# One-head attention layer: denominators, scores and masked weights placed on other engines

## The chip, the core and the metric

The kernel runs on one core of a Trainium2 chip. The metric is device time in microseconds, taken as the median of several runs. A profiled execution is one more execution, recorded by the hardware profiler; its own time is given beside that of the runs.

The engines' names in the profile: PE is TensorE (matmul), PEld its weight loads, DVE is VectorE, ACT is ScalarE, POOL is GpSimd, and SP is the engine that issues most of the plain transfers.

## The reference

Four graph attention layers follow one another on 3327 nodes with 512 features. Each is residual: `x = x + GAT(relu(layernorm(x)))`. The layers have 8, 4, 1 and 8 heads. The one that matters here is the third, with one head:

```python
h = features @ W                       # 512 x 512
s1, s2 = h @ a1, h @ a2                # own score, neighbour's score
e = leaky_relu(s1[:, None] + s2[None, :], 0.2)
e = where(adjacency > 0, e, -9e15)
h_prime = softmax(e, axis=1) @ h
out = elu(h_prime)
```

The adjacency matrix is the same in all layers and sparse: about 17 neighbours per node, with a tail of nodes that have more.

## The kernel before, in words

**Tiling.** Nodes are padded to 3328 and ranked by their number of neighbours, so that they make 26 tiles of 128 nodes (`NT = 26`). A first stage reads the adjacency matrix, finds each node's neighbours and their ranks, and computes the first layer's features. Then the four layers run in `tile_gat_lists`. Each keeps a table in HBM, with one row of 528 numbers for each node: the features, its own score and its neighbour's score.

**Two ways of averaging.** In the one-head layer the nine tiles with most neighbours are *dense*: class `Wholes` treats all 26 source tiles for three target tiles at a time (`wide` is 384 columns), in three rounds `p` with 26 source tiles `j` each. The other 17 are *list* tiles: class `Tile` gathers the rows of the neighbours by indirect DMA from POOL (`gather`, line 835), in groups of up to four (`GROUP`), and VectorE accumulates the weighted rows (line 912).

**A list tile's group.** `fetch` issues the gathers, five groups ahead (`LOOK = 5`, and as many buffers g). `scored` makes the weights: at a tile's first group the own score is copied into `self.s` (line 886); then VectorE adds it to the neighbours' scores (line 888) and takes the leaky relu (line 890), and ScalarE the exponential (line 891). `group` accumulates. After a tile's last group come `divisors`, `means`, and then the tile's end (`ends`): ELU in `bent` and `added` (lines 948 to 964), centring and squares on ScalarE (970, 973), the root on POOL (431), transposes (451), the projection onto the next layer's weights (469), and the table row's store.

**A dense source tile.** Since exp of a leaky relu is the larger of two exponentials, the weight of a source j for a target c is `c_j * max(b_j/c_j * a_c, 1)` up to a factor of the target. The code computes it as a relu with a scale and a bias, plus a constant:

```python
r = self.r[p, j] = pools["o"].tile([P, wide], F32, name="r")                    # PSUM, one buffer
nc.scalar.activation(r, self.a[p], AF.Relu, scale=b, bias=mc)                   # line 1128
...
nc.vector.scalar_tensor_tensor(self.e[p, j], self.r.pop((p, j)), self.c[:, j:j + 1],
                               self.mk.pop((p, j)), OP.add, OP.mult)            # line 1135
```

Then `products` multiplies the masked weights em with the source tile's features on TensorE (line 1162), into one PSUM bank for each of the three target tiles. The denominators take another way: POOL adds two masked weight tiles (`paired`, line 1148), VectorE folds one or two such pairs into a running sum (`added`, line 1154), and after the last source tile TensorE multiplies the sum by a column of ones (`divisors`, line 1169). `means` takes the reciprocal (1173), and `Whole.means` scales the three banks (1089).

**What sets the order.** The engines' instruction order in the layers is written out by hand: a loop over steps (one per list group, 72 in this layer) in which pieces are put with `later(step, place, piece)`. A step has the places "first", "scored" (with the next group's scores), then the group itself, then "last". `Wholes.place` spreads the 26 source tiles of a round over 19 of 21 steps, so that some steps hold two. Each engine executes its own instructions in this order. The transfers by SP are in the order of the same pieces, except that they wait for their buffers.

The functions that the change touches, and what calls them:

Of the kernel before, what the change touches and what calls it, by code (L numbers as in the profile page):

```python
# [10 lines left out]
F32 = mybir.dt.float32  # L11
U8 = mybir.dt.uint8
BF16 = mybir.dt.bfloat16
I32 = mybir.dt.int32
AF = mybir.ActivationFunctionType
OP = mybir.AluOpType
AX = mybir.AxisListType

P = 128
SLOPE = 0.2  # L20
# [5 lines left out]
BANK = 512  # L26
# [8 lines left out]
ROW = 528  # L35
GROUP = 4
DENSE = [0, 1, 9, 3]
ND = max(DENSE)
# [342 lines left out]
class Weights:  # L381
# [19 lines left out]
    def fold(self):  # L401

        if not self.left:
            return
        nc, HF = self.nc, self.HF
        s, k = self.left.pop(0)
        prod = self.work.tile([P, 2 * HF], F32, name="prod", bufs=1)
        nc.vector.tensor_mul(prod.rearrange("p (s n) -> p s n", s=2), self.w[:, k, :, :HF],
                             self.av[:, s, :].rearrange("p (s n) -> p s n", s=2))
        nc.vector.tensor_reduce(self.w[:, k, s, HF:HF + self.H],  # L410
                                prod.rearrange("p (h d) -> p h d", d=self.D), AX.X, OP.add)


def centred(nc, xt, small, work):
# [382 lines left out]
def tile_gat_lists(ctx: ExitStack, tc: tile.TileContext, x, adj, ws, avs, out, ident, half, slots, L, low, spare, tabx, tabs):  # L797
# [7 lines left out]
    nc = tc.nc  # L805
    NP, F = x.shape
    NT = NP // P
# [15 lines left out]
    wide = 3 * P  # L823
# [5 lines left out]
    one, zero = [spool.tile([P, 1], F32, name=n, bufs=1) for n in ("one", "zero")]  # L829
# [16 lines left out]
    class Tile:  # L846
# [29 lines left out]
        def scored(self, i):  # L876

            H = HEADS[self.l]
            t = self.t
            k0, n, g = self.groups[i]  # L880
            if i == 0:
                self.po = pools["o"].tile([P, BANK], F32, name="bank")
                pw = next(scores)
                K = CAPS[t]
                self.wt, self.s = pw[:, :K * 8].rearrange("p (k h) -> p k h", h=8), pw[:, K * 8:K * 8 + H]
                nc.vector.tensor_copy(self.s, g[:, n, F:F + H] if self.l == 0 else g[:, 0, F // 2:F // 2 + H])
            z = small.tile([P, GROUP, 8], F32, name="z")[:, :n, :H]
            nc.vector.tensor_tensor(z, g[:, :n, ROW - 8:ROW - 8 + H],  # L888
                                    self.s.unsqueeze(1).to_broadcast([P, n, H]), OP.add)
            nc.vector.scalar_tensor_tensor(z, z, SLOPE, z, OP.mult, OP.max)  # L890
            nc.scalar.activation(self.wt[:, k0:k0 + n, :H], z, AF.Exp)  # L891
            if self.l == 0:
                ranks = n - (i == 0)
                nc.scalar.activation(slots(t, max(k0, 1), count=ranks), g[:, :ranks, F // 2], AF.Copy)
                if i == 0:
                    nc.scalar.activation(xs[self.t], g[:, n, :F], AF.Copy)
# [30 lines left out]
        def divisors(self):  # L927
            H, K = HEADS[self.l], CAPS[self.t]
            den = self.den = small.tile([P, 8], F32, name="den")
            nc.vector.tensor_reduce(den[:, :H], self.wt[:, :K, :H].rearrange("p k h -> p h k"), AX.X, OP.add)  # L930
            nc.vector.tensor_scalar_max(den[:, :H], den[:, :H], TINY)
            nc.vector.reciprocal(den[:, :H], den[:, :H])
# [151 lines left out]
    class Whole(Tile):  # L1084


        def means(self):
            self.y = low[:, self.t % 3 * F:(self.t % 3 + 1) * F]
            nc.vector.tensor_scalar(self.y, self.po, self.den, None, OP.mult)

    class Wholes:


        def __init__(self, l, W):
            self.l, self.tiles = l, [Whole(l, t, W) for t in range(ND)]
            self.s = pools["e"].tile([P, ND], F32, name="s", bufs=1)
            for t in range(ND):
                nc.sync.dma_start(self.s[:, t:t + 1], tabs[l % 2][t * P:(t + 1) * P, F // 2:F // 2 + 1])
            self.b, self.c, self.mc = [pools["e"].tile([P, NT], F32, name=n, bufs=1) for n in ("b", "c", "mc")]

            self.a = [low[:, 5 * F + p % 2 * wide:5 * F + (p % 2 + 1) * wide] for p in range(ND // 3)]
            self.v, self.e, self.mk, self.r, self.pairs, self.parts = {}, {}, {}, {}, {}, {}

        def targets(self, p):

# [4 lines left out]
            nc.scalar.activation(self.a[p], pa[:, :3, :], AF.Exp, scale=1.0 - SLOPE)  # L1110

        def load(self, p, j):
            v = self.v[p, j] = pools["e"].tile([P, ROW], F32, name="ve", bufs=4)
            nc.sync.dma_start(v, tabs[self.l % 2][j * P:(j + 1) * P, :])
            mk = self.mk[p, j] = pools["e"].tile([P, wide], U8, name="mk", bufs=3)
            nc.sync.dma_start(mk.bitcast(I32), masks[p, j])

        def weights(self, p, j):
            if p == ND // 3:
                return  # L1120
            b, c, mc = [t[:, j:j + 1] for t in (self.b, self.c, self.mc)]
            if p == 0:
                d = self.v[p, j][:, ROW - 8:ROW - 7]
                nc.scalar.activation(b, d, AF.Exp)
                nc.scalar.activation(c, d, AF.Exp, scale=SLOPE)
                nc.scalar.activation(mc, c, AF.Copy, scale=-1.0)
            r = self.r[p, j] = pools["o"].tile([P, wide], F32, name="r")
            nc.scalar.activation(r, self.a[p], AF.Relu, scale=b, bias=mc)

        def masked(self, p, j):  # L1130

            if j % 2 == 0:
                self.two = pools["e"].tile([P, 2, wide], F32, name="em", bufs=3)
            self.e[p, j] = self.two[:, j % 2, :]
            nc.vector.scalar_tensor_tensor(self.e[p, j], self.r.pop((p, j)), self.c[:, j:j + 1],  # L1135
                                           self.mk.pop((p, j)), OP.add, OP.mult)
            if j % 2:
                self.pairs[p, j // 2] = self.two

        def part(self, p, i):  # L1140
            if (p, i) not in self.parts:
                self.parts[p, i] = pools["e"].tile([P, 3, wide], F32, name="parts", bufs=2)
            return self.parts[p, i]

        def paired(self, p, i):

            two = self.pairs.pop((p, i))
            nc.gpsimd.tensor_tensor(self.part(p, i // 2)[:, 1 + i % 2, :], two[:, 0, :], two[:, 1, :], OP.add)

        def added(self, p, i):  # L1150

            parts = self.part(p, i // 2)[:, i < 2:2 + i % 2, :]
            out_ = self.a[p] if i == NT // 2 - 1 else self.part(p, i // 2 + 1)[:, 0, :]
            nc.vector.tensor_reduce(out_, parts.rearrange("p j c -> p c j"), AX.X, OP.add)

        def products(self, p, j):
            e, v = self.e.pop((p, j)), self.v.pop((p, j))
# [5 lines left out]
                                 v.rearrange("p (s m) -> p s m", s=2)[:, :, :F // 2],  # L1163
                                 start=(j == 0), stop=(j == NT - 1))

        def divisors(self, p):
            self.pd = pools["t"].tile([P, F // P, P], F32, name="pt")
            for q in range(3):
                nc.tensor.matmul(self.pd[:, 0, q:q + 1], self.a[p][:, q * P:(q + 1) * P], one, start=True, stop=True)

        def means(self, p):
            den = small.tile([P, 3], F32, name="den3")
            nc.vector.reciprocal(den, self.pd[:, 0, :3])
            for q in range(3):
                tl = self.tiles[3 * p + q]
                tl.den = den[:, q:q + 1]
                tl.means()

        def place(self, n):

            per = n // (ND // 3)
            for p in range(ND // 3):
                s0 = p * per
                later(s0 - 4 if p else -1, "first", lambda p=p: self.targets(p))
                for j in range(NT):
                    s = s0 + j * (per - 2) // NT
                    later(max(s - 3, -1), "first", lambda p=p, j=j: self.load(p, j))

                    if (p, j) == (0, 0):
                        later(-1, "scored", lambda: self.weights(0, 0))  # L1190
                    later(s, "first", lambda p=p, j=j: (self.masked(p, j), self.weights(*divmod(p * NT + j + 1, NT))))
                    later(s + 1, "first", lambda p=p, j=j: self.products(p, j))
                    if j % 2:
                        i = j // 2
                        later(s + 1, "first", lambda p=p, i=i: self.paired(p, i))
                        if i % 2 or j == NT - 1:
                            later(s + 2, "last", lambda p=p, i=i: self.added(p, i))
                later(s + 3, "first", lambda p=p: self.divisors(p))
                later(s + 3, "last", lambda p=p: self.means(p))
                for q in range(3):  # L1200
                    self.tiles[3 * p + q].ends(s + 3 + q)
# [149 lines left out]
    def later(s, place, piece):  # L1351
        at.setdefault((s, place), []).append(piece)
# [128 lines left out]
```

## Time and profile before

| what | value |
|---|---|
| median of three runs | 2442.68 us (2439.82 to 2448.11) |
| the profiled execution's own time | 2959.5 us |
| its span, first to last instruction | 2957.8 us |
| mean granted TensorE clock | 0.867 |
| TensorE, VectorE, ScalarE, POOL busy in the whole span | 2224.7, 1914.3, 931.8, 1728.5 us |
| accumulation in the one-head layer (line 912), first to last start | 1861.8 to 2277.4 us |
| dense products in it (line 1162), first to last start | 1858.9 to 2230.4 us |

The profiled execution takes longer than the runs. Durations below come from it alone. A line of groups gives the source line, engine, operation, output and inputs, shapes and count; after the first bar the busy time of the group in us and the mean of one in ns; after the second the idle time of the engine just ahead of these instructions and what ended it. An fp32 matmul appears as two records. A line of waits reads "who waited <- for whom: us in total, times, longest".

### The profile page before, as it was taken

The numbers are of one execution on the slowest core, as the hardware profiler recorded it, in microseconds if no ns is written. First come the engines' busy times: TensorE is split into PE (matmuls) and PEld (weight loads), VectorE is DVE, ScalarE is ACT, GpSimd is POOL, SyncE is SP. The second block draws the span as 40 slices with busy tenths as digits, with TensorE's granted clock in tenths as the row PEclk, the third lists the DMA queues.
The fourth block names the chain that finished last, engine by engine and source line by source line (L and its number), as shares of the span: only waits on it lengthen the run. The fifth ranks groups of instructions, "written<-read, shape, count | busy, mean of one in ns | idle before, by whom it ended". The sixth has DMA issues, their size and how long they took to land.

```text
span 2957.8 us, 27080 instructions
## 1 busy us (share of the span) xinstructions
PE 2224.7 (75%) x7082; PEld 1251.4 (42%) x7082; DVE 1914.3 (65%) x4968; ACT 931.8 (32%) x2502; POOL 1728.5 (58%) x1717
## 2 busy tenths in 40 slices
PE   4777677787677745788877787689696778877887
PEld 2664243343333323344434344245354445444453
DVE  7887656565546523767765565698887556666665
ACT  5882122222221101323332222344333333333330
POOL 7894465565556663555655552676764555555554
PEclk9988788888888877899988889799897889988898
DMA  6885477677666675666766663788775666666664
GB/s 229 322 294 160 140 218 216 193 235 222 188 205 195 189 194 170 181 202 192 209 193 189 192 192 111 226 264 257 236 248 152 191 177 184 185 182 194 185 187 137
DMA packets 260730, 594.20 MB, mean 201 GB/s; under 512 B 103699, under 2 KB 121107, under 8 KB 256214
## 3 DMA queue, kind: packets, MB, share of 16 engines
q0 software_dynamic: 124368, 432.13, 49.8%
q1 hardware_dynamic: 132454, 153.45, 16.5%
q10 hardware_dynamic: 3744, 6.82, 0.7%
q8 instruction: 57, 0.93, 0.1%
q14 instruction: 107, 0.88, 0.1%
HBM read 542.60 MB, written 49.65 MB: 200 GB/s over the span
## 4 chain that ended last, share of the span: by engine, by line
DVE 21%; PE 18%; issue 16%; another core or an unknown queue 11%; ACT 6%; POOL 4%; DMA 3%; DVEq 0%; ACTq 0%; POOLq 0%; SPq 0%
PE bank L924 11%; DVE m L919 9%; POOL g L835 3%; PE pv L469 3%; PE whole L1310 3%; DVE bank L912 2%; DMA g<-tab,idxb 1%; DVE z L890 1%; DVE z L888 1%; ACT r L1276 1%; DVE x L962 1%; DVE q L439 1%; ACT pw L891 1%; DVE room L1292 1%
## 5 line engine op out<-in xcount | busy, mean ns | idle before, releaser
L924 PE MATMUL bank<-m,ident 128*128 128x512 f32 x2414 | 1236.5, 659 | 268.9 <-DVE m L919 137.5
L835 POOL DMA_INDIRECT g<-tab,idxb x712 | 678.2, 952 | 465.5 <-issue 189.3
L919 DVE TENSOR_TENSOR m<-g,pw 128x512 f32<-128x512 f32 x1207 | 752.0, 682 | 267.6 <-ACT pw L891 193.5
L924 PEld LDWEIGHTS bank<-m,ident 128*128 128x128 f32 x2414 | 490.2, 211 | 879.8 <-issue 568.9
L469 PE MATMUL pv<-w,hT 128*128 128x264 f32 x1664 | 447.4, 423 | 107.0 <-ACT hT L458 71.2
L835 POOL DMA_INDIRECT g<-tabx,twiceb x342 | 324.1, 948 | 245.8 <-issue 124.4
L835 POOL DMA_INDIRECT g<-tab,idxa x297 | 283.1, 953 | 262.1 <-DMA tab<-v 88.5
L469 PEld LDWEIGHTS pv<-w,hT 128*128 128x128 f32 x1664 | 339.5, 208 | 215.2 <-ACT hT L458 79.6
L891 ACT ACTIVATE pw<-z 128x32 f32<-128x32 f32 (+4 forms) x356 | 67.8, 190 | 945.4 <-DVE z L890 509.8
L1162 PE MATMUL whole<-ve,em 128*128 128x512 f32 x468 | 224.5, 632 | 48.2 <-DVE em L1135 27.9
L1310 PE MATMUL whole<-L,room 128*128 128x130 f32 x1248 | 171.1, 288 | 79.2 <-issue 79.0
L1310 PEld LDWEIGHTS whole<-L,room 128*128 128x128 f32 x1248 | 163.1, 201 | 107.1 <-issue 104.7
L695 POOL TENSOR_TENSOR key<-a,keys 128x3328 int32<-128x3328 int32 (+1 forms) x29 | 189.5, 6539 | 15.9 <-DVE cand L704 12.6
L912 DVE SCALAR_TENSOR_TENSOR bank<-g,L,bank 128x512 f32<-128x512 f32 x243 | 183.3, 754 | 9.9 <-remote 2.0
L835 POOL DMA_INDIRECT g<-tabx,twicea x99 | 94.4, 954 | 119.6 <-issue 75.3
L1162 PEld LDWEIGHTS whole<-ve,em 128*128 128x128 f32 x468 | 92.8, 203 | 158.7 <-issue 114.6
L451 PE MATMUL pt<-ident,xn 128*128 128x128 f32 x416 | 74.5, 302 | 93.0 <-issue 32.2
L704 DVE MAX8 cand<-key 128x8 f32<-128x208 int32 x416 | 143.6, 363 | 0.1
L890 DVE SCALAR_TENSOR_TENSOR z<-z 128x32 f32<-128x32 f32 (+5 forms) x428 | 82.5, 193 | 91.4 <-remote 61.4
L919 DVE TENSOR_TENSOR bank<-g,pw 128x512 f32<-128x512 f32 x74 | 51.5, 696 | 126.7 <-ACT pw L891 105.6
L1276 ACT ACTIVATE r<-low,L 128x384 f32<-128x384 f32 x208 | 121.2, 582 | 9.8 <-remote 3.9
L888 DVE TENSOR_TENSOR z<-g,pw 128x32 f32<-128x32 f32 (+4 forms) x356 | 61.8, 174 | 94.9 <-DMA g<-tab,idxa 39.0
(181 smaller groups left out, 2154.4 us busy)
## 6 DMA issues: line engine op xcount, KB each, us to landing
a<-in_adj SPq DMA_DIRECT2D x25, 1664.0 KB
tab<-v SPq DMA_DIRECT2D x78, 264.0 KB
ve<-tab SPq DMA_DIRECT2D x78, 264.0 KB
g<-tab SPq DMA_DIRECT2D x65, 264.0 KB
tabx<-vx SPq DMA_DIRECT2D x26, 528.0 KB
g<-tab,idxb POOLq DMA_INDIRECT x712
low<-tab SPq DMA_DIRECT2D x52, 132.0 KB
spare<-tab SPq DMA_DIRECT2D x52, 132.0 KB
```

The source lines that it names most:

```text
L469: nc.tensor.matmul(pv[:, s, :HF + 8], hT[:, k, :], W.w[:, k, s, :], start=(k == 0), stop=(k == KC - 1))
L695: nc.gpsimd.tensor_tensor(key[:, c:c + quarter], a[:, c:c + quarter], keys[:, c:c + quarter], OP.mult)
L704: nc.vector.max(cand[:, g * 8:(g + 1) * 8], key[:, g * SEG:(g + 1) * SEG])
L835: nc.gpsimd.indirect_dma_start(out=out_, out_offset=None, in_=table, in_offset=bass.IndirectOffsetOnAxis(ap=which, axis=0))
L890: nc.vector.scalar_tensor_tensor(z, z, SLOPE, z, OP.mult, OP.max)
L891: nc.scalar.activation(self.wt[:, k0:k0 + n, :H], z, AF.Exp)
L912: nc.vector.scalar_tensor_tensor(acc, v, w, acc, OP.mult, OP.add)
L919: nc.vector.tensor_tensor(out_.rearrange("p (s h d) -> p s h d", s=2, d=D), v.rearrange("p s (h d) -> p s h d", d=D), wt[:, k0 + q, :H].re ...
L924: nc.tensor.matmul(self.po, ident, m[:, q, :], start=False, stop=(k0 + q == K - 1), skip_group_check=True)
L1162: nc.tensor.matmul(tl.po.rearrange("p (s m) -> p s m", s=2), e[:, q * P:(q + 1) * P], v.rearrange("p (s m) -> p s m", s=2)[:, :, :F // 2], ...
L1276: nc.scalar.activation(self.r[:, h, :], self.a[:, g, :], AF.Relu, bias=-1.0, scale=self.b[:, j, g:g + 1])
L1310: nc.tensor.matmul(dst, e[:, h, q * P:(q + 1) * P], mov, start=False, stop=(j == NT - 1), skip_group_check=True)
```

## The change

There are six edits. All but the first are in the one-head layer.

- When the weights of that layer are folded, a second score column is made beside each: the neighbour's score times 0.2 and the own score times 0.8. The factor `exp(0.2 * own)` cancels in the softmax, so the leaky relu becomes one operation, `max(s2 + 0.8*s1, 0.2*s2)`. It replaces two.
- The copy of the own score goes from VectorE to ScalarE.
- `Whole.means` goes from VectorE to ScalarE.
- ScalarE writes the dense weights straight into the SBUF pairs em (four pairs, where there were three), and VectorE adds and masks them in place. The PSUM buffer r is gone.
- VectorE's running sums are gone. Each pair sum from POOL is multiplied by the column of ones on TensorE, and accumulates in a PSUM bank of its own, which takes the place of r.
- Rows and masks of a source tile are loaded four steps ahead and not three, with five buffers each (four and three before).

```diff
@@ fold
+        if self.H == 1:
+            nc.vector.tensor_scalar(self.w[:, k, s, HF + 1:HF + 2], self.w[:, k, s, HF:HF + 1],
+                                    SLOPE if s else 1.0 - SLOPE, None, OP.mult)
@@ scored
-                nc.vector.tensor_copy(self.s, g[:, n, F:F + H] if self.l == 0 else g[:, 0, F // 2:F // 2 + H])
+                if H == 1:
+                    nc.scalar.activation(self.s, g[:, 0, F // 2 + 1:F // 2 + 2], AF.Copy)
+                else:
+                    nc.vector.tensor_copy(self.s, g[:, n, F:F + H] if self.l == 0 else g[:, 0, F // 2:F // 2 + H])
             z = small.tile([P, GROUP, 8], F32, name="z")[:, :n, :H]
+            if H == 1:
+
+                nc.vector.scalar_tensor_tensor(z, g[:, :n, ROW - 8:ROW - 7], self.s, g[:, :n, ROW - 7:ROW - 6],
+                                               OP.add, OP.max)
+                nc.scalar.activation(self.wt[:, k0:k0 + n, :H], z, AF.Exp)
+                return
@@ Whole.means
-            nc.vector.tensor_scalar(self.y, self.po, self.den, None, OP.mult)
+            nc.scalar.activation(self.y, self.po, AF.Copy, scale=self.den)
@@ Wholes.__init__
+            bank = pools["o"].tile([P, BANK], F32, name="pd")
+            self.pd = [bank[:, 8 * p:8 * p + 3] for p in range(ND // 3)]
@@ load
-            v = self.v[p, j] = pools["e"].tile([P, ROW], F32, name="ve", bufs=4)
+            v = self.v[p, j] = pools["e"].tile([P, ROW], F32, name="ve", bufs=5)
...
-            mk = self.mk[p, j] = pools["e"].tile([P, wide], U8, name="mk", bufs=3)
+            mk = self.mk[p, j] = pools["e"].tile([P, wide], U8, name="mk", bufs=5)
@@ weights, masked
-            r = self.r[p, j] = pools["o"].tile([P, wide], F32, name="r")
-            nc.scalar.activation(r, self.a[p], AF.Relu, scale=b, bias=mc)
+            if j % 2 == 0:
+                self.made = pools["e"].tile([P, 2, wide], F32, name="em", bufs=4)
+            self.e[p, j] = self.made[:, j % 2, :]
+            nc.scalar.activation(self.e[p, j], self.a[p], AF.Relu, scale=b, bias=mc)
+            if j % 2:
+                self.pairs[p, j // 2] = self.made
...
+            e = self.e[p, j]
+            nc.vector.scalar_tensor_tensor(e, e, self.c[:, j:j + 1], self.mk.pop((p, j)), OP.add, OP.mult)
@@ paired, added
-            nc.gpsimd.tensor_tensor(self.part(p, i // 2)[:, 1 + i % 2, :], two[:, 0, :], two[:, 1, :], OP.add)
+            self.sums[p, i] = pools["e"].tile([P, wide], F32, name="sums", bufs=3)
+            nc.gpsimd.tensor_tensor(self.sums[p, i], two[:, 0, :], two[:, 1, :], OP.add)
...
-            nc.vector.tensor_reduce(out_, parts.rearrange("p j c -> p c j"), AX.X, OP.add)
+            both = self.sums.pop((p, i))
+            for q in range(3):
+                nc.tensor.matmul(self.pd[p][:, q:q + 1], both[:, q * P:(q + 1) * P], one, start=(i == 0 and q == 0),
+                                 stop=(i == NT // 2 - 1), skip_group_check=True)
@@ divisors (removed), means
-                nc.tensor.matmul(self.pd[:, 0, q:q + 1], self.a[p][:, q * P:(q + 1) * P], one, start=True, stop=True)
...
-            nc.vector.reciprocal(den, self.pd[:, 0, :3])
+            nc.vector.reciprocal(den, self.pd[p])
@@ place
-                    later(max(s - 3, -1), "first", lambda p=p, j=j: self.load(p, j))
+                    later(max(s - 4, -1), "first", lambda p=p, j=j: self.load(p, j))
...
-                        if i % 2 or j == NT - 1:
-                            later(s + 2, "last", lambda p=p, i=i: self.added(p, i))
-                later(s + 3, "first", lambda p=p: self.divisors(p))
+                        later(s + 3, "first", lambda p=p, i=i: self.added(p, i))
                 later(s + 3, "last", lambda p=p: self.means(p))
```

More of the change, by code (lines that the diff above doesn't have):

```diff
@@ L1101, in __init__ @@
             self.a = [low[:, 5 * F + p % 2 * wide:5 * F + (p % 2 + 1) * wide] for p in range(ND // 3)]
-            self.v, self.e, self.mk, self.r, self.pairs, self.parts = {}, {}, {}, {}, {}, {}
+            self.v, self.e, self.mk, self.pairs, self.sums = {}, {}, {}, {}, {}
+            bank = pools["o"].tile([P, BANK], F32, name="pd")
+            self.pd = [bank[:, 8 * p:8 * p + 3] for p in range(ND // 3)]
         def targets(self, p):
@@ L1126, in weights @@
                 nc.scalar.activation(mc, c, AF.Copy, scale=-1.0)
-            r = self.r[p, j] = pools["o"].tile([P, wide], F32, name="r")
-            nc.scalar.activation(r, self.a[p], AF.Relu, scale=b, bias=mc)
-        def masked(self, p, j):
[L1132 to L1143, printed above, removed]
+            if j % 2 == 0:
[4 more added lines that the diff above has]
+                self.pairs[p, j // 2] = self.made
+        def masked(self, p, j):
+            e = self.e[p, j]
+            nc.vector.scalar_tensor_tensor(e, e, self.c[:, j:j + 1], self.mk.pop((p, j)), OP.add, OP.mult)
         def paired(self, p, i):
             two = self.pairs.pop((p, i))
-            nc.gpsimd.tensor_tensor(self.part(p, i // 2)[:, 1 + i % 2, :], two[:, 0, :], two[:, 1, :], OP.add)
+            self.sums[p, i] = pools["e"].tile([P, wide], F32, name="sums", bufs=3)
+            nc.gpsimd.tensor_tensor(self.sums[p, i], two[:, 0, :], two[:, 1, :], OP.add)
         def added(self, p, i):
-            parts = self.part(p, i // 2)[:, i < 2:2 + i % 2, :]
-            out_ = self.a[p] if i == NT // 2 - 1 else self.part(p, i // 2 + 1)[:, 0, :]
-            nc.vector.tensor_reduce(out_, parts.rearrange("p j c -> p c j"), AX.X, OP.add)
+            both = self.sums.pop((p, i))
+            for q in range(3):
+                nc.tensor.matmul(self.pd[p][:, q:q + 1], both[:, q * P:(q + 1) * P], one, start=(i == 0 and q == 0),
+                                 stop=(i == NT // 2 - 1), skip_group_check=True)
         def products(self, p, j):
@@ L1164, in products @@
                                  start=(j == 0), stop=(j == NT - 1))
-        def divisors(self, p):
-            self.pd = pools["t"].tile([P, F // P, P], F32, name="pt")
-            for q in range(3):
-                nc.tensor.matmul(self.pd[:, 0, q:q + 1], self.a[p][:, q * P:(q + 1) * P], one, start=True, stop=True)
         def means(self, p):
             den = small.tile([P, 3], F32, name="den3")
-            nc.vector.reciprocal(den, self.pd[:, 0, :3])
+            nc.vector.reciprocal(den, self.pd[p])
             for q in range(3):
```

## The prediction

> **What bounds the kernel now.** The edits lie in the third of four layers (the one with one head) and in a fold of its weights, so I first cut that layer out. The engine sums by stretch show it: it starts when the last rows of its table have landed (about 1850 us), its vector work ends near 2285. The next layer cannot begin its gathers before, so what ends this layer earlier ends the kernel earlier by as much.
>
> ```profile
> core 0: us, PE busy (x) PEld busy (x) DVE busy (x) ACT busy (x) POOL busy (x), PEclk, DMA share, GB/s
> 1850.00:2285.00 435.00, 338.70 (x1004) 191.68 (x1005) 358.67 (x728) 169.40 (x410) 289.15 (x307) 0.89 0.77 235
> ...
> 2020.00:2060.00 40.00, 40.00 (x134) 24.14 (x135) 32.05 (x64) 15.68 (x32) 25.78 (x28) 1.00 0.88 272
> 2140.00:2180.00 40.00, 40.00 (x142) 25.68 (x141) 30.26 (x63) 16.10 (x32) 25.05 (x28) 1.00 0.75 233
> 2100.00:2120.00 20.00, 9.97 (x33) 6.21 (x34) 18.56 (x36) 6.08 (x14) 10.14 (x11) 0.76 0.68 201
> 2240.00:2260.00 20.00, 9.42 (x31) 7.40 (x32) 17.95 (x45) 8.46 (x20) 14.15 (x16) 0.67 0.66 177
> ```
>
> VectorE is busy 359 of 435 us, TensorE 339, ScalarE 169. Two kinds of stretch alternate: where three dense tiles end (2100, 2240) VectorE is full and TensorE half idle at a low clock; after the first of these ends (2020, 2140) TensorE is full, catching up, and VectorE waits. POOL's 289 hides the pause between gathers, which is why I count it by hand. Next, the groups of the layer's window, for durations and counts:
>
> ```profile
> L1162 PE MATMUL whole<-ve,em 128*128 128x512 f32 x468 | 224.5, 632 | 48.2 <-DVE em L1135 27.9 <-issue 13.9 <-DVE low L1089 6.4
> L912 DVE SCALAR_TENSOR_TENSOR bank<-g,L,bank 128x512 f32<-128x512 f32 x243 | 183.3, 754 | 9.9 <-remote 2.0 <-DVE bank L912 1.2
> ...
> L1135 DVE SCALAR_TENSOR_TENSOR em<-r,c,mk 128x384 f32<-128x384 f32 x78 | 47.8, 612 | 24.8 <-issue 10.1 <-ACT r L1128 8.5 <-ACT hT L458 4.8
> L1148 POOL TENSOR_TENSOR parts<-em 128x384 f32<-128x384 f32 x39 | 39.3, 1007 | 0.8
> L1154 DVE TENSOR_REDUCE parts<-parts 128x384 f32<-128x1152 f32 x15 | 22.0, 1467 | 0.0
> ...
> L1089 DVE TENSOR_SCALAR low<-whole,den 128x512 f32<-128x512 f32 x9 | 6.2, 744 | 0.1
> ```
>
> TensorE waits for the masked weights (L1135), and these stand in VectorE's queue behind reductions (L1154) that nothing needs before the tiles end. Last, the waits, to see who holds whom:
>
> ```profile
> ACT r L1128 <- DVE em L1135: 75.2, 36, 5.5
> ```
> ```profile
> POOL root L431 <- DVE ve L978: 33.8, 12, 8.3
> ...
> POOL g L835 <- DVE bank L912: 13.1, 9, 3.4
> ```
>
> ScalarE waits 75 us for its single PSUM buffer r; POOL waits for VectorE. Both point at VectorE as the pace.
>
> **POOL's floor.** In the timeline a gather takes 0.95 us and the next follows 0.30 later. The layer has 243: 304 us. Its 39 pair sums at 1.00 + 0.17 are 46, its 26 roots at 0.56 + 0.17 are 19. Sum 369. The gathers run from 1849.3 to 2264.7, 415 us. So POOL has 46 us of slack, spent on waits for VectorE; no relief of VectorE alone can bring more than that in the profiled execution.
>
> [...] with one PSUM operand L912 takes 756 ns, with two SBUF operands L962 takes 692, both on 512 elements. [...] The masked weights become such an operation. [...] L956, with two SBUF inputs, has a median of 690 ns with one case of 2108, the gathers a median near 950 with a maximum of 1364. [...]
>
> **The change part by part**, against the profiled execution's own 2959.5 us.
>
> *Running sums.* 21 reductions leave VectorE: 22.0 + 2.9 + 2.9 (18 and 3 of them, 1.47 us wide and 0.95 narrow) = 27.8 us. In their place TensorE multiplies each of 39 pair sums by ones, three products each, and nine at the ends go: 36 groups of three more. The nine in the trace (L1169) took 0.80 us per three at the full clock and 1.41 at a low one. So TensorE gains 29 to 51 us; I take 29, because they fall mostly in busy stretches. That is work on an engine with 96 us idle, but in the 80 us where TensorE is full it is paid: 80/435 of 29, 5 us.
>
> *Scores.* 72 groups lose one of two small operations. Their median is 157 ns (L888), start to start 0.2: 11 to 14 us off VectorE, taken as 11. The own-score copy (17 at 144 ns) goes to ScalarE: 2.4 us off.
>
> *Dense means.* Nine at 0.69 to 0.74 us: 6.2 us off VectorE. ScalarE gets nine at about 0.70 (its L476, from PSUM with a scale) and 17 small copies at 0.19: 9.5 us on an engine 39% busy. If that cover were gone the next tile's first product would be late by 2 us, three times.
>
> *Weights into SBUF pairs.* ScalarE no longer waits for r. VectorE idled 8.5 us on r and 10.1 unexplained before L1135, chiefly when one step holds two source tiles; I count 12 of these 19. Duration of the in-place operation: by the 64 ns above, 5 us less over 78; [...] taking L956's mean of 795 over its median, 8 us more. I take nothing. ScalarE's write to SBUF is not in the trace in this form; against the present 675 ns its neighbours to SBUF give 614 to 706 for 512 elements, so between -5 and +5 us on an engine with room.
>
> *Loads.* The same 78 rows and 78 masks, issued one step earlier with five buffers of each. On SP's queue a row load still waits for a product about three steps before its use, and own rows and table stores behind it wait no longer. ScalarE waits 27.9 us on rows, 13.6 of it once at the start, which an earlier issue does not move as they hang on the table. Nothing counted.
>
> *New waits.* TensorE's small products stand at step s + 3, products of later source tiles behind them; they wait for POOL's pair sum of step s + 1. VectorE had this wait before at s + 2, and lost 2.1 us in 21 reductions. *Folds:* eight operations of about 0.15 us in the first layer, 1.2 us, beside TensorE's sums there.
>
> *Sum.* VectorE: 27.8 + 11 + 2.4 + 6.2 = 47.4 busy, 12 idle, 59 in all. Only the 355 of 435 us in which TensorE is not full can profit: 48; less 5 for the added products: 43. POOL's slack of 46 cannot be used whole, since each root still waits for VectorE and each gather for a buffer; three quarters of 43 is 32. This quarter is my judgement. What is late next: POOL at 369 and TensorE at 339 + 29 = 368, both in about 400.
>
> So 2959.5 becomes about 2927. The median of the runs is 2442.7, 517 us less than the profiled execution; the trace doesn't say where. Shrunk by that ratio, the layer would have 359 us, exactly VectorE's busy time, so VectorE is there at least as much the bound. I take off the same 32 us, unscaled: 2410.
>
> **Rivals.** (a) *POOL or TensorE takes over at once.* If POOL's pauses and waits stay, or the added products cost 51 us, 10 to 18 us remain: about 2428. For it: TensorE would be 92% busy. Against it: its clock rises as it fills. (b) *The layer runs free,* if unprofiled gathers are quicker: 47 busy plus all 19 idle, less 8 for TensorE: 2385. (c) *Slower: TensorE held by POOL.* A gather step puts four gathers (5 us) and perhaps a root ahead of the pair sum. If POOL stands more than two steps (2 x 5.9 us) behind TensorE, each of 39 small groups holds the products, then SP's row loads, then the masks. TensorE has 96 - 29 = 67 us of idle left: a mean hold over 1.7 us decides. At 2.4 us, 39 x 2.4 - 67 = 27 us slower: 2470. Against it: the 2.1 us of before, at one step less distance; for it: a faster VectorE brings TensorE closer to POOL. (d) *It doesn't do what it says:* relief goes to waits on table rows or ELU inputs (L956 waits 11.2 us for ScalarE), no change, 2440.
>
> **How the numbers follow.** Forecast (20 to 45 us gained) 0.50; (a) 0.19; (b) 0.08; (d) 0.09; (c) 0.14. A change under 0.3%, 7 us, is about what a measurement here cannot tell from none. Faster 0.77, within 0.09, slower 0.14. The forecast's own range is 2397 to 2423. The range 2385 to 2446 takes in (a), (d) and the edge of (b), and leaves out most of (c) and the rest of (b), under 0.2.
>
> **What would show it.** Right: in the layer VectorE's busy time is near 311 us, the wait of ScalarE for em under 10, gathers end 25 to 45 us earlier, POOL's waits for L978 shrink, small products near 0.13 us each, TensorE's clock above 0.89. Wrong: TensorE waiting for POOL's sums by tens of us (c); gathers ending as late as before with POOL never idle (a); masked weights above 0.7 us or gathers above 1.0 [...].

## The result, and the profile after

The changed kernel takes 2420.86 us (median of five runs, 2419.54 to 2423.97) and the kernel before 2440.68 (median of five). The ratio is 0.9916, with a 95% interval of 0.9903 to 0.9928. That is 20 us faster. A later set of runs gave 2422.32 against 2441.29, 0.9927 (0.9911 to 0.9943).

One thing has to be cleared before traces are compared. The profiled execution that the prediction started from took 2959.5 us, its runs 2442.7. The profile after took as long as its runs. So the kernel before was profiled again (first experiment), with a span of 2438.4 us, and all readings of "before" from here on are from that profile.

The one-head layer is cut from its first gather to the last table row that ScalarE writes (in the profiles of the changed kernel, and of some experiments, from the second gather, 1.25 us later). First the kernel before, profiled again, then the changed kernel (engine sums by stretch: us busy and number of instructions, then TensorE's granted clock, the share of DMA, GB/s):

```profile
core 0: us, PE busy (x) PEld busy (x) DVE busy (x) ACT busy (x) POOL busy (x), PEclk, DMA share, GB/s
1500.43:1926.90 426.47, 342.18 (x1022) 194.73 (x1022) 357.77 (x730) 170.56 (x414) 290.17 (x308) 0.90 0.77 240
```
```profile
1501.90:1907.50 405.60, 353.28 (x1238) 214.92 (x1236) 323.53 (x612) 178.69 (x440) 300.61 (x307) 0.93 0.81 252
...
1660.00:1680.00 20.00, 20.00 (x85) 14.23 (x83) 13.10 (x22) 5.76 (x13) 16.23 (x18) 1.00 0.94 293
1680.00:1700.00 20.00, 20.00 (x67) 10.98 (x67) 14.04 (x29) 7.90 (x17) 15.65 (x17) 1.00 0.89 280
...
1780.00:1800.00 20.00, 20.00 (x77) 13.07 (x76) 10.59 (x20) 6.22 (x13) 10.61 (x12) 1.00 0.74 233
```

The layer is 20.9 us shorter (426.5 to 405.6; 19.6 from the first gather of each), about as much as the whole span (2438.4 to 2417.8). VectorE lost 34 us of work and not 47, and it idles 82 us in the layer where it idled 69; POOL's same instructions got 10 us longer; TensorE gained 11, although it has 36 groups of small products more: the products with the features took 612 ns and not 629 (L1173 below, L1162 before), at a granted clock of 0.93 where it had been 0.90. In the stretches where TensorE is full, VectorE idles a third to a half of the time: the pace there has passed to TensorE. These stretches have grown: in slices of 20 us, counted from the first gather, TensorE is full for 80 us of the layer before and for 180 us of it after.

The groups that changed, in the changed kernel (output and inputs, shapes, count, busy us, mean ns; then idle before and its releasers):

```profile
L1173 PE MATMUL whole<-ve,em 128*128 128x512 f32 x468 | 217.8, 612 | 16.3 <-DVE em L1152 11.2 <-ACT low L1101 5.2
...
L838 POOL DMA_INDIRECT g<-tab,idxb x144 | 145.0, 1007 | 45.3 <-issue 33.1 <-DVE bank L924 4.2 <-ACT L L898 2.7
...
L1152 DVE SCALAR_TENSOR_TENSOR em<-em,c,mk 128x384 f32<-128x384 f32 x78 | 56.7, 740 | 23.1 <-ACT em L1145 14.7 <-issue 8.3
L1145 ACT ACTIVATE em<-low,mc,b 128x384 f32<-128x384 f32 x78 | 53.2, 699 | 1.6 <-ACT mc L1141 0.4
...
L1164 PE MATMUL pd<-one,sums 128*128 128x1 f32 x234 | 30.2, 245 | 16.3 <-POOL sums L1158 16.3
...
L434 POOL TENSOR_TENSOR root<-ve,half 128x1 f32<-128x1 f32 x26 | 19.0, 732 | 19.9 <-DVE pw L892 14.3 <-DVE ve L990 5.4
```

Their counterparts in the kernel before, profiled again:

```profile
L1162 PE MATMUL whole<-ve,em 128*128 128x512 f32 x468 | 223.4, 629 | 36.6 <-DVE em L1135 30.2 <-DVE low L1089 6.4
...
L1135 DVE SCALAR_TENSOR_TENSOR em<-r,c,mk 128x384 f32<-128x384 f32 x78 | 47.7, 612 | 26.5 <-ACT r L1128 26.5
```
```profile
L835 POOL DMA_INDIRECT g<-tab,idxb x144 | 139.9, 971 | 54.4 <-issue 35.5 <-DVE bank L912 9.6 <-DVE den L931 3.7
...
L431 POOL TENSOR_TENSOR root<-ve,half 128x1 f32<-128x1 f32 x26 | 15.9, 611 | 42.7 <-DVE ve L978 20.0 <-DVE pw L886 15.8 <-DVE z L888 6.9
```

The masked weights (L1152) have a mean of 740 ns where the kernel before had 612; the gathers 1007 where it had 971; the roots 732 where it had 611.

The longer mean of the masked weights comes from a few of them. Their median is 614 ns, where it was 611. Ten of the 78 met one of POOL's pair sums in time; these took 1.16 to 2.11 us, and each ended 0.43 us after its pair sum did. The other 68 took at most 0.67 us. In the kernel before, where one input lies in PSUM, 12 met a pair sum, and none took more than 0.62 us. One of the ten (start and length in us):

```profile
1823.96 1.70 DVE L1152 SCALAR_TENSOR_TENSOR em<-em,c,mk 128x384 f32<-128x384 f32 x1
1824.23 1.00 POOL L1158 TENSOR_TENSOR sums<-em 128x384 f32<-128x384 f32 x1
```

TensorE now waits 16.3 us for POOL's pair sums (who waited <- for whom: us, times, longest):

```profile
PE pd L1164 <- POOL sums L1158: 16.3, 6, 5.5
```

ScalarE waits no longer for the weights' buffer: it idles 1.6 us ahead of all 78. Its waits moved to the scores, from 47.8 us to 124.4 ahead of the exponential. VectorE's idle time ahead of the masked weights fell only from 26.5 to 23.1 us. The waits for the buffer in the kernel before:

```profile
ACT r L1128 <- DVE em L1135: 125.9, 57, 5.5
```
```profile
DVE em L1135 <- ACT r L1128: 26.5, 22, 5.1
```

### The profile page after: what moved, and what is told of

Same layout as the page of the kernel before. It is cut to its first block, busy times and chain, and to the rows that moved or that the text cites. A ratio compares the mean times of both kernels' runs of the same rounds, so it can differ in the third digit from the quotient of the medians.

```text
span 2417.8 us, 27489 instructions
## 1 busy us (share of the span) xinstructions
PE 2068.3 (86%) x7298; PEld 1197.0 (50%) x7298; DVE 1885.1 (78%) x4857; ACT 936.3 (39%) x2528; POOL 1739.5 (72%) x1717
## 3 DMA queue, kind: packets, MB, share of 16 engines
q1 hardware_dynamic: 132454, 153.45, 19.6%
## 4 chain that ended last, share of the span: by engine, by line
DVE 31%; DMA 17%; PE 16%; issue 13%; POOL 12%; ACT 9%; DVEq 0%; SPq 0%; ACTq 0%; POOLq 0%
DVE m L931 13%; POOL g L838 8%; DMA g<-tab,idxb 6%; PE bank L936 5%; DMA g<-tabx,twiceb 4%; PE pv L472 4%; PE whole L1173 3%; POOL key L698 3%; DVE bank L924 3%; ACT r L1280 2%; DMA g<-tab,idxa 2%; DVE room L1296 2%; DVE z L902 2%; ACT pw L903 2%; DVE z L900 1%
## 5 line engine op out<-in xcount | busy, mean ns | idle before, releaser
L936 PE MATMUL bank<-m,ident 128*128 128x512 f32 x2414 | 1128.0, 613 | 144.8 <-DVE m L931 144.3
L936 PEld LDWEIGHTS bank<-m,ident 128*128 128x128 f32 x2414 | 448.7, 194 | 689.2 <-issue 314.6
L472 PE MATMUL pv<-w,hT 128*128 128x264 f32 x1664 | 431.5, 413 | 67.8 <-ACT hT L461 44.5
L472 PEld LDWEIGHTS pv<-w,hT 128*128 128x128 f32 x1664 | 331.7, 203 | 166.8 <-ACT hT L461 50.8
L1173 PE MATMUL whole<-ve,em 128*128 128x512 f32 x468 | 217.8, 612 | 16.3 <-DVE em L1152 11.2
L698 POOL TENSOR_TENSOR key<-a,keys 128x3328 int32<-128x3328 int32 (+1 forms) x29 | 189.3, 6530 | 16.3 <-DVE cand L707 11.8
L1314 PEld LDWEIGHTS whole<-L,room 128*128 128x128 f32 x1248 | 147.5, 190 | 24.9 <-issue 19.1
L1314 PE MATMUL whole<-L,room 128*128 128x130 f32 x1248 | 147.8, 274 | 0.0
L1173 PEld LDWEIGHTS whole<-ve,em 128*128 128x128 f32 x468 | 88.1, 196 | 109.2 <-issue 87.2
L454 PE MATMUL pt<-ident,xn 128*128 128x128 f32 x416 | 65.4, 281 | 35.4 <-ACT hT L461 13.6
L454 PEld LDWEIGHTS pt<-ident,xn 128*128 128x128 f32 x416 | 52.5, 145 | 68.6 <-issue 28.3
```

The costliest lines, as they stand in the source:

```text
L454: nc.tensor.transpose(pt[:, k, :], xn[:, k * P:(k + 1) * P], ident)
L472: nc.tensor.matmul(pv[:, s, :HF + 8], hT[:, k, :], W.w[:, k, s, :], start=(k == 0), stop=(k == KC - 1))
L698: nc.gpsimd.tensor_tensor(key[:, c:c + quarter], a[:, c:c + quarter], keys[:, c:c + quarter], OP.mult)
L936: nc.tensor.matmul(self.po, ident, m[:, q, :], start=False, stop=(k0 + q == K - 1), skip_group_check=True)
L1173: nc.tensor.matmul(tl.po.rearrange("p (s m) -> p s m", s=2), e[:, q * P:(q + 1) * P], v.rearrange("p (s m) -> p s m", s=2)[:, :, :F // 2], ...
L1314: nc.tensor.matmul(dst, e[:, h, q * P:(q + 1) * P], mov, start=False, stop=(j == NT - 1), skip_group_check=True)
```

## Experiments

Four theories were set against each other. A: the gain is VectorE's relief, the running sums first. B: it is the second buffer between ScalarE and VectorE. C: after the change TensorE is the bound, so that work moved to it is paid in full. D: POOL's gathers are at their floor of 369 us, so that more relief elsewhere brings nothing.

**The kernel before once more.** No edit.

> The kernel before, unchanged, profiled once more, because its first profiled execution took 517 us longer than the runs while that of the changed kernel took as long as its runs. If that was this one execution, the span is now near 2439 us, the one-head layer shorter than 435 us (about 420 to 425, since the change gained 20 and has about 402), gathers at the same pitch of 1.25 us, VectorE busy about 359 us in the layer. If the kernel before is really recorded more slowly, the span is again near 2950.

It took 2440.14 us with a span of 2438.4. So the long profiled execution does not belong to the kernel. The last four experiments landed on a second chip, on which the kernel before takes 2941.77 us (median of 56 runs), with a granted clock near 0.87, as in that first profile. So the difference goes with the chip, or with its state at that hour; which chip the first profile ran on is not known. In the first profile the one-head layer took 444.1 us where it takes 426.5 here, so only 18 of the 517 us lay in it. In that profile ScalarE waited 109.1 us for something unknown ahead of one line of the eight-head layers (L1287), here none; on the second chip the same line waits 107.1 us in the run with the loads as before. What is slow there was not settled.

**Running sums back on VectorE.**

```diff
-            for q in range(3):
-                nc.tensor.matmul(self.pd[p][:, q:q + 1], both[:, q * P:(q + 1) * P], one, ...)
+            nc.vector.tensor_reduce(out_, parts.rearrange("p j c -> p c j"), AX.X, OP.add)
...
```

> The changed kernel with the running sums back on VectorE and the nine products at the ends; all else as changed. Theory A (VectorE's relief is the gain, its largest part the 27.8 us of sums, and TensorE's 30 us of small products eat part of it): 2431 to 2437, 10 to 16 slower than changed. Theory B (the gain comes from the second buffer between ScalarE and VectorE): within 5 us of the changed kernel, 2416 to 2426. Theory C (TensorE is the bound after the change, the sums cost as much on it as they freed): 2410 to 2420.

2423.95 us, ratio to before 0.9914 (0.9902 to 0.9927): the same ratio as the whole change. The sums edit, which was the largest term of the prediction, is worth nothing that can be measured beside the others; the two intervals leave about 4 us either way (an estimate from their widths). Theory A fails for its main part; the time lies in B's range. Beside this run and the two that follow, the kernel before took 2444.11 us, 3.4 more than beside the changed kernel, so their ratios say more than their times: this one gives 2420 us of the 2440.68 that the expectations stood on, in B's range still and at the edge of C's.

```profile
1502.03:1912.90 410.87, 337.10 (x1022) 193.00 (x1022) 346.68 (x633) 178.05 (x440) 300.08 (x308) 0.91 0.80 249
```

VectorE has 23 us more work than in the changed kernel, TensorE 16 less, and the layer is 4 us longer in this one profile, from the first gather of each.

**A single buffer between ScalarE and VectorE.** As its PSUM bank now holds the denominators, it lies in SBUF.

```diff
-            self.e[p, j] = self.made[:, j % 2, :]
-            nc.scalar.activation(self.e[p, j], self.a[p], AF.Relu, scale=b, bias=mc)
+            r = self.r[p, j] = pools["e"].tile([P, wide], F32, name="r", bufs=1)
+            nc.scalar.activation(r, self.a[p], AF.Relu, scale=b, bias=mc)
...
-            nc.vector.scalar_tensor_tensor(e, e, self.c[:, j:j + 1], self.mk.pop((p, j)), OP.add, OP.mult)
+            nc.vector.scalar_tensor_tensor(e, self.r.pop((p, j)), self.c[:, j:j + 1], self.mk.pop((p, j)),
+                                           OP.add, OP.mult)
```

> The changed kernel, but ScalarE writes the weights to one single SBUF buffer and VectorE from there into the pairs, so that the wait for this buffer is back while the sums stay on TensorE. Theory A: 12 us of VectorE's idle come back, some hidden: 2424 to 2430. Theory B: most of the 20 us is lost: 2434 to 2441.

2433.99 us, ratio 0.9956 (0.9944 to 0.9969). About half of the gain is gone, 10 us: more than A allowed and, by a hair, less than B asked. By its ratio it would be 2430 us of the same 2440.68, at A's upper end. So B is at most half right.

```profile
1502.69:1919.00 416.31, 360.28 (x1238) 218.61 (x1236) 329.63 (x612) 178.69 (x440) 299.80 (x307) 0.92 0.80 245
...
L1150 DVE SCALAR_TENSOR_TENSOR em<-r,c,mk 128x384 f32<-128x384 f32 x78 | 62.4, 800 | 31.1 <-issue 16.2 <-ACT r L1143 12.4 <-POOL root L434 2.5
```

Nor are these 10 us the wait alone. VectorE's idle time ahead of the masked weights grew from 23.1 to 31.1 us, but the operations themselves grew too, from 740 to 800 ns, as 16 of them and not ten met a pair sum. VectorE has 6 us more work in a layer that is 10.7 us longer. How much of the 10 us is the wait stays open.

**Scores in two operations, own-score copy and dense means back on VectorE.**

```diff
-                nc.vector.scalar_tensor_tensor(z, g[:, :n, ROW - 8:ROW - 7], self.s, g[:, :n, ROW - 7:ROW - 6],
-                                               OP.add, OP.max)
+            nc.vector.tensor_tensor(z, g[:, :n, ROW - 8:ROW - 8 + H], ..., OP.add)
+            nc.vector.scalar_tensor_tensor(z, z, SLOPE, z, OP.mult, OP.max)
...
-            nc.scalar.activation(self.y, self.po, AF.Copy, scale=self.den)
+            nc.vector.tensor_scalar(self.y, self.po, self.den, None, OP.mult)
```

> The changed kernel with scores in two operations, own-score copy and dense means back on VectorE, 20 us more VectorE work (11 + 2.4 + 6.2). Theory A (VectorE still sets the pace where TensorE is not full): 2428 to 2434. Theory D (POOL's gathers at 369 us are already the floor, VectorE has room): 2419 to 2424.

2434.0 us, ratio 0.9954 (0.9939 to 0.9970). Again about half of the gain is gone, 10 us, for 14 us of VectorE's work in the profile (337.50 busy against 323.53).

```profile
1503.50:1921.50 418.00, 358.96 (x1236) 217.53 (x1234) 337.50 (x709) 172.11 (x414) 300.69 (x307) 0.92 0.79 244
```

The layer is 12.4 us longer than the changed kernel's. So VectorE still sets the pace in much of the layer, as A has it and not D. The three parts were put back together, and which of them carries the 10 us is not shown. That the last two runs make up the whole gain need not mean that their parts add: no run put both back.

The next three ran together, with the changed kernel as their measure.

> The changed kernel, unchanged, as the measure for the three that follow on the same chip: 2419 to 2424.

It gave 2422.32 us, and a layer of 406.1 us.

```profile
1503.66:1909.80 406.14, 354.17 (x1238) 216.22 (x1236) 321.60 (x612) 178.85 (x440) 300.13 (x307) 0.93 0.82 251
```

**Few small products.** 36 of the 39 groups are left out, the others multiply the target factors; POOL still makes its sums.

```diff
-            both = self.sums.pop((p, i))
+            self.sums.pop((p, i))
+            if i < NT // 2 - 1:
+                return
...
```

> The changed kernel with 36 of its 39 groups of small products left out; the three that stay multiply the target factors and not the sums, so the denominators are not those of the reference. POOL makes its pair sums as before, nobody waits for them. Theory C (TensorE is the bound after the change): 30 us of products and 16 us of waits for POOL go, 2400 to 2412. Theory D (POOL is at its floor: in the changed profile its gathers run without a real pause, 383 us against a counted 369 plus about 10 of stretching): within 4 us of the changed kernel.

2408.43 us, ratio to before 0.9861 (0.9842 to 0.9881), 14 us faster than the changed kernel. So the small products, with their waits, cost 14 us at the end. Theory C holds.

```profile
1503.32:1896.10 392.78, 329.79 (x1022) 191.14 (x1022) 322.50 (x612) 178.35 (x440) 300.81 (x308) 0.93 0.83 260
```

From the first gather of each the layer is 15 us shorter than in the measure, with VectorE and POOL as busy as there. From the first gather to the end of the last it takes 369.6 us (1503.32 to 1872.93), where the changed kernel takes 384.2 and the kernel before 398.8. The prediction had counted POOL's floor at 369. By its timeline POOL has next to no other pause here: its gaps of more than 0.32 us between these gathers make 2.1 us, against 17.2 in the changed kernel. So D comes next, right behind C.

**No pair sums on POOL.** TensorE multiplies both tiles of a pair.

```diff
-            nc.gpsimd.tensor_tensor(self.sums[p, i], two[:, 0, :], two[:, 1, :], OP.add)
+            self.sums[p, i] = two
...
+                for h in range(2):
+                    nc.tensor.matmul(self.pd[p][:, q:q + 1], both[:, h, q * P:(q + 1) * P], one, ...)
...
-                        later(s + 3, "first", lambda p=p, i=i: self.added(p, i))
+                        later(s + 1, "first", lambda p=p, i=i: self.added(p, i))
```

> The changed kernel without POOL's pair sums: TensorE multiplies both weight tiles of a pair by the column of ones, 78 groups of small products where there were 39, two steps earlier. POOL loses 46 us of work, TensorE gains another 30. Theory D: faster than the changed kernel, by 5 to 20 us, 2400 to 2415. Theory C: slower by 5 to 20, 2425 to 2440.

2435.6 us, ratio 0.9972 (0.9963 to 0.9982), 13 us slower than the changed kernel although POOL has 43 us less to do, VectorE 17, and TensorE does not wait for pair sums at all. The stretch shows why:

```profile
1504.86:1922.40 417.54, 378.05 (x1472) 240.72 (x1471) 304.26 (x612) 178.70 (x440) 257.54 (x268) 0.94 0.79 245
...
L1164 PE MATMUL pd<-one,em 128*128 128x1 f32 x468 | 54.4, 243 | 0.0
```

24 us more of small products (30.2 to 54.4) make the layer 11 us longer, with no wait ahead of them: they cost as work, though by about half of what they take and not in full. Theory C again for the bound; D's gain does not appear while TensorE holds the pace.

**Pair sums on VectorE.**

```diff
-            nc.gpsimd.tensor_tensor(self.sums[p, i], two[:, 0, :], two[:, 1, :], OP.add)
+            nc.vector.tensor_tensor(self.sums[p, i], two[:, 0, :], two[:, 1, :], OP.add)
...
-                        later(s + 3, "first", lambda p=p, i=i: self.added(p, i))
+                        later(s + 2, "first", lambda p=p, i=i: self.added(p, i))
```

> The changed kernel with the 39 pair sums made by VectorE (about 0.56 us each, 22 us) and not by POOL, and the small products one step earlier. POOL loses 46 us. Theory D: faster by 8 to 20 us, 2400 to 2413, if VectorE has the room. Theory A (VectorE still sets the pace): slower by 8 to 15, 2429 to 2436. Theory C: within 5 us.

2416.24 us, ratio 0.9898 (0.9884 to 0.9913); the changed kernel beside it 0.9927 (0.9911 to 0.9943). That is 6 us faster, between what D and C asked, and the two intervals still touch. It is the fastest whole version that was run, but its lead over the changed kernel is likely rather than established. Its groups tell more than its time:

```profile
L1152 DVE SCALAR_TENSOR_TENSOR em<-em,c,mk 128x384 f32<-128x384 f32 x78 | 46.6, 613 | 20.0 <-ACT em L1145 20.0
...
L1158 DVE TENSOR_TENSOR sums<-em 128x384 f32<-128x384 f32 x39 | 21.4, 549 | 0.0
```

Without POOL's pair sums the masked weights fall to 613 ns, from 730 in the measure, and the small score operations of the widest groups (L896) from 303 to 223. So VectorE, with 21.4 us of new work, is no busier in the layer than in the measure (321.65 against 321.60 us). The other runs agree on the masked weights: 615 ns where nobody adds the pairs (the run before this one), 654 where POOL makes 18 additions (the last run below), and 705 to 800 in each run of the changed kernel or a variant of it in which POOL makes all 39.

The last four ran together on the second chip told of above, without the changed kernel beside them. There, the runs spread more, and each says only how it stands to the kernel before on that chip.

**Loads as before** (three steps ahead, four and three buffers).

> The changed kernel with the loads as before: three steps ahead, four row buffers, three mask buffers. As predicted (the earlier loads are worth nothing): 2419 to 2425. If the loads carry part of the gain, since the row load on SP's queue waits for a product and the masks stand behind it: 2427 to 2434.

**All small products, on the target factors,** so that nothing waits for POOL.

> The changed kernel with all 39 groups of small products in their places, but on the target factors and not on the pair sums, so that TensorE's work stays and its wait for POOL goes; the denominators are not those of the reference. If the small products cost the 14 us shown by their removal as work: 2418 to 2423. If they cost it as a wait for POOL (16 us of it in the changed profile): 2407 to 2413.

**VectorE adds two pair sums,** TensorE has 21 groups.

> The changed kernel with VectorE adding two pair sums at a time (18 additions of about 0.56 us, 10 us), so that TensorE has 21 groups of small products and not 39: TensorE loses 14 us, VectorE gains 10. If TensorE is the closest bound: 2412 to 2419. If VectorE is as close, no gain: 2420 to 2426.

**VectorE makes the pair sums, POOL adds two of them,** TensorE has 21 groups.

> VectorE makes the 39 pair sums (22 us), POOL adds two of them at a time (18 of 1.17 us, 21 us; it had 46), TensorE has 21 groups of small products (14 us less). If TensorE and POOL are the close bounds and VectorE has room: 2403 to 2412, faster than the pair sums on VectorE alone. If the longer chain from VectorE over POOL to TensorE makes TensorE wait: 2416 to 2424.

```
                               median    ratio to before (95%)
loads as before                2929.55   0.9945 (0.9921 to 0.9970)
products without the wait      2920.57   0.9938 (0.9904 to 0.9972)
quads on VectorE               2931.56   0.9973 (0.9951 to 0.9994)
quads on POOL                  2922.20   0.9908 (0.9877 to 0.9940)
```

All the expected times were for the other chip and can't be held against these. The ratio of the changed kernel (0.9916 and 0.9927 elsewhere) lies inside or at the edge of the first two and the last; only the quads on VectorE are apart from it, on the slower side. (If the changed kernel gained its 20 us here too, its ratio would be 0.993, which no run shows; the reading stays the same.) The products without the wait gain 21 us, by the interval 8 to 28, about what the changed kernel gains elsewhere and less than the 33 us of the run with few products. That points to work rather than wait, as the run without pair sums does, but without the changed kernel on this chip it is no proof. So whether the earlier loads are worth anything, and whether the 14 us of the small products are work or wait, stay open, and none of the four is shown to beat the changed kernel.

## Why the prediction was right, and where its sum was not

The direction and the range held: 2410 was forecast, with 2385 to 2446, and 2420.86 was measured. The gain is 20 us where the sum said 32. The mechanism, relief of VectorE until TensorE and POOL are as late, is in the main what the runs show: work put back on VectorE costs time, small products taken from TensorE give 14 us, and POOL reaches its floor right behind. The sum was wrong in its parts. By its own factors it gave some 13 us to the running sums, 12 to the scores, copy and means, and 7 to the buffer; undone one at a time these were worth 0, 10 and 10. That the total came within 11 us owes something to luck. Term by term:

- **Running sums, 27.8 us off VectorE less 5 for the added products.** This is the term that was mis-sized. The edit is worth nothing measurable (0.9914 with it undone against 0.9916). The small products did take 0.13 us each (30.2 us for 234 records), as counted. But they cost 14 us at the end, not 5. The share of full TensorE time was read off the old kernel, 80 of 435 us, in slices of 20 us. Counted so, TensorE is full for 180 us in the changed kernel, and for 120 with few small products, where VectorE's relief is left. The slice matters as well: in slices of 5 us the first profile itself has 230 us of full TensorE in the layer's 444, and the same sum would have given 15 us.
- **In-place weights at no cost.** The prediction had this between 5 us less and 8 us more and took 0. Measured: the mean went from 612 to 740 ns, 10 us over 78, a little beyond the upper end, nearly all of it in the ten that met a pair sum. The 8 us were L956's mean over its median, 795 and 690 ns, times 78. In that profile two of L956's 26 cases, 2001 and 2108 ns (the prediction saw one), are just the two that met a pair sum, while the masked weights met 12. The price to count was that of a meeting: 1.3 and 1.4 us over the median there, 1.0 us in the changed kernel. Of the predicted 47.4 us off VectorE these 10 are most of what is missing from the measured 34.
- **The buffer's wait, 12 us of idle.** The single buffer cost 10 us, but part of that is longer operations, and from before to after VectorE's idle time ahead of the masked weights fell by 3 us only. So the size is not confirmed. The first profile had 8.5 us of this wait and some unexplained, the one taken again 26.5.
- **Scores, copy and means, 20 us of work.** Put back, they brought 14 us of work and cost 10. The single score operation took 304 ns for the widest groups, where the two had 223 and 220; in all, the scores saved 9.8 us of the 11 counted.
- **POOL's floor, 369 us.** Right: with few small products the gathers took 369.6. In the changed kernel they take 384.2, and the small products are what holds them: of the two that the prediction saw as next late, POOL and TensorE, TensorE comes first.
- **Discount of a quarter.** A judgement. The two terms that counted come to 26 us before it and 19 after it, beside the 20 measured; that it fits does not show its reasons, POOL's waits for VectorE and for buffers, to be the cause.
- **517 us between profile and runs.** Taking the gain unscaled was right: they are not the kernel's, and the layer held only 18 of them. The argument beside it, that VectorE would fill the shrunk layer, was empty.
- **Rivals.** (a), TensorE takes over at once, is the one that came true in part: 2428 was its time, and the result lies between it and the forecast, nearer to (a). (c), TensorE held by POOL, shows as 16.3 us of waits in 6 cases, 0.4 us for each of 39 small groups where it needed 1.7 to decide.
- **The signs named beforehand.** ScalarE's wait for em is gone, POOL's waits for the squares (L978, L990 after) fell from 20.0 to 5.4 us, and the clock is 0.93 where above 0.89 was named, though it was 0.90 before as well. VectorE's busy time is 323.5 us where 311 was named, and the gathers end 15 us earlier (398.8 to 384.2 from the first one) where 25 to 45 was. Of the last two signs, masked weights above 0.7 us came clearly, at 0.74 in the mean; gathers above 1.0 only just, at 1.00 in the mean, where they were 0.97 before.

## What to carry to other kernels

In this kernel, work taken off the busiest engine was worth what the next engine left of it. So price the receiving engine at the load it will have after the change, not at the one in the old profile. Undoing the parts one at a time showed where the gain hangs: half of it goes with the single buffer, half with the group of scores, copy and means, and none with the largest edit, which moved a cost from one full engine to another. And price operations that grow when they meet another engine's by how often they meet (here ten of 78, 1.0 us for each), not by a mean. And before a profile is read against runs of another time, see that both took equally long.

## What was not expected of the hardware

- An in-place VectorE operation with two SBUF inputs was no faster than the same with one input in PSUM: medians of 614 and 612 ns on 384 elements. The 64 ns that the prediction's neighbours on 512 elements had shown (756 against 692) did not carry over.
- With two SBUF inputs, each of the ten such operations that met one of POOL's additions of 1.0 us ended 0.43 us after it, after up to 2108 ns, and the mean rose by 20%. POOL's additions stayed at 1.0 us (1007 ns before and after). Without these additions the mean was 613 ns. With one input in PSUM, 12 meetings cost nothing (at most 619 ns).
- The gathers' mean rose by some 3% (971 to 1007 ns), and most of that stayed without the additions (997 with the pair sums on VectorE). Why is open.
- The same kernel took 2441 to 2444 us on one chip and 2942 on another.
